# A graph layer with convolutions: output, hT and graph sums stored from GpSimd's queue, first batch's messages read in place

## The chip, the cores and the metric

The kernel runs on one core of one Trainium2 chip. The time is device microseconds (us) of one execution. The kernel before took a median of 2251.97 us over three runs (2245.11 to 2256.61). A profile is one further execution; all its numbers are that execution's.

The core's engines each work through their own list of instructions in order: TensorE (PE, matrix products; its weight loads are shown as PEld), VectorE (DVE), ScalarE (ACT), GpSimd (POOL) and SyncE (SP, which here only issues transfers). A transfer (DMA) is issued by an engine's queue and then moved by 16 DMA engines that all queues share.

## The reference

Input is x (32 batches of 512 nodes with 256 features) and an adjacency mask for each batch. Cut to what matters:

```python
h = maximum(layernorm(x), 0)                       # per node; h is called hT in the kernel, features on partitions
# inside the layer, with x = h:
c  = relu(conv1d(h, conv1_w, width 1) + bn1)
c  = conv1d(c, conv2_w, width 17) + bn2
x_conv = relu(c + h)
s   = h @ w_se.T + b_se                            # 3 numbers per node
A   = exp(-dist(s, s)) * adj
msg = relu(h @ w_msg.T + b_msg)
x_nmp = A @ msg                                    # the "graph sums"
gi = concat(x_conv, x_nmp) @ w_ih.T + b_ih
gh = h @ w_hh.T + b_hh
r, z = sigmoid(gi_r + gh_r), sigmoid(gi_z + gh_z)
n = tanh(gi_n + r * gh_n)
out = x + (1 - z) * n + z * h
```

## The kernel before, in words

All is float32. Work is divided into five streams, written as Python generators, and one planner that keeps a modelled clock `now` and, at each step, takes the next piece of the stream that is furthest behind its share. What a stream yields is the modelled time at which its next piece may go. The order in which pieces are taken is the order in which every engine's list is written; on the chip only semaphores hold an engine back.

- `begin(b)` and `norm`: layer-normalise x of batch b. DVE makes the statistics, GpSimd raises them to the power -0.5 (`rstd`, line 216), DVE makes `shift`, ACT applies both. Then `norm_t` turns the result by TensorE into hT, and stores hT to a DRAM tile (`HD`, shown as `hd`, line 318) from ACT's queue. Every later use of hT, except conv1 of the first four batches, loads it back on SP's queue: `hT` for conv1 (line 172), `hTg` for the messages (line 177), `hTb` for the gates (line 183).
- `rows(b)`: conv1, and its result into `h1` for a group of four batches (G = 4). A group's rows can be made only when the operands of the group before have been taken from `h1`.
- `convolution`: conv2 as 25 products per group of four batches, with transformed weights. These are kept in DRAM (`wd`) and loaded again for each group (`w`, line 469, three buffers).
- `graph(b)`: messages (`messages`), the factors of the distance, the exponential, the mask (`masked`; its rows of adj are loaded as `m_sb`, four transfers of 64 KB for each 128 rows from batch 8 on, line 264), and `gather`, which forms the graph sums and stores them to DRAM (`nd`, line 760) from ACT's queue.
- `gates(b)`: the gate products, and at the end `leave`, which turns the result, adds x (`res`, loaded by line 772) and stores the output in four transfers per half (line 892), from SP's queue. Each of them writes 32 partitions x 16 runs of 32 numbers (128 B).

Four facts about order matter below. First, each list is worked in order: while SP waits for one transfer's semaphore, every load behind it waits too. Second, every transfer is given one of eight semaphores in turn, `DMAHW0` to `DMAHW7` for those issued from SP and ACT together, `DMASW0` to `DMASW7` for those issued from GpSimd, and it waits until the transfer that had this semaphore last has landed. So a load on SP can be held by a store on ACT that stands some eight transfers earlier in the program, even if ACT has not reached that store yet. Third, `load` times in the planner are constants: it takes 6 us for a load of weights or rows. Fourth, at the start `graph(0)` loads `hTg` back from DRAM before the first messages can be formed.

Lines 127 and 132 are the helpers through which all products and turns by TensorE go, line 118 the one for DVE and ACT; they are told apart by tile names.

Of the kernel before, what the change touches and what calls it, by code (L numbers as in the profile page):

```python
# [44 lines left out]
def kernel(  # L45
# [28 lines left out]
    nc = tc.nc  # L74
# [23 lines left out]
    now = 5.0  # L98
    LAG = 0.6
# [22 lines left out]
    dve, act = Engine(nc.vector, 0.12, 0.00108), Engine(nc.scalar, 0.16, 0.0009)  # L122
# [6 lines left out]
    def turn(ps, a):  # L129
        nonlocal now  # L130
        now += 0.11
        nc.tensor.transpose(ps, a, ident)  # L132

    def matmul_sum(ps, pairs):
        for i, (lhsT, rhs) in enumerate(pairs):
            matmul(ps, lhsT, rhs, start=(i == 0), stop=(i == len(pairs) - 1))

    def bank():
        return gps.tile([P, N], F32, name="ps_g")
# [4 lines left out]
    def later(t, f):  # L144
        LATER.append((t, f))
        LATER.sort(key=lambda e: e[0])

    def settle():
        while LATER:
            LATER.pop(0)[1]()  # L150


    XS, HT, HB, HR, HG, XN, XR = {}, {}, {}, {}, {}, {}, {}
    NORMS, NORM_AT = {}, {}
    ARRIVES = (0.0, 7.0, 11.0, 13.0)
    HD = {b: dram.tile([P, ND, N], F32, name=f"hd{b}") for b in range(B)}
    ND_ = {(b, d): dram.tile([P, N], F32, name=f"nd{b}_{d}") for b in range(B) for d in range(ND)}
    begun = 0

    def fetch(b, xs=None):  # L160
        XS[b] = front.tile([P, NT, D], F32, name="x_sb", bufs=2) if xs is None else xs
# [2 lines left out]
    def load(b, xs=None):  # L164
        if b not in XS:
            fetch(b, xs)
        NORMS[b] = norm(b)
        NORM_AT[b] = now + 7.0 if b >= G else ARRIVES[b]

    def load_row(b):  # L170
        HR[b] = front.tile([P, ND, N], F32, name="hT", bufs=2)
        nc.sync.dma_start(HR[b], HD[b])

    def load_graph(b):
        if b < B and b not in HG and begun > b:
            HG[b] = front.tile([P, ND, N], F32, name="hTg", bufs=1)
            nc.sync.dma_start(HG[b], HD[b])
# [33 lines left out]
    def rsqrt(dst, var):  # L211

        n = dst.shape[-1]
        t = front.tile([P, 4], F32, name="veps")
        dve.tensor_scalar(t[:, :n], var, EPS, None, op0=ALU.add)
        nc.gpsimd.tensor_tensor(dst, t[:, :n], mhalf[:, :n], op=ALU.pow)
# [56 lines left out]
    def norm(b):  # L273

        xs = XS[b]
        st = front.tile([P, NT, 6], F32, name="st")
        mv = front.tile([P, NT, 2], F32, name="mv")
        for c in range(NT):
            dve.bn_stats(st[:, c, :], xs[:, c, :])
            dve.bn_aggr(mv[:, c, :], st[:, c, :])  # L280
            if c % 2:
                yield 0.0
        rstd = front.tile([P, NT], F32, name="rstd")
        rsqrt(rstd, mv[:, :, 1])
        yield dve.free + 1.5
        shift = front.tile([P, NT], F32, name="shift")
        dve.scalar_tensor_tensor(
            shift, mv[:, :, 0], -1.0, rstd, op0=ALU.mult, op1=ALU.mult
        )
        yield dve.free + 0.2  # L290
        for c in range(NT):
            act.activation(
                xs[:, c, :], xs[:, c, :], AF.Identity, bias=shift[:, c : c + 1],
                scale=rstd[:, c : c + 1],
            )
            if c % 2:
                yield act.free + LAG
# [10 lines left out]
    def norm_t(b, d):  # L308
        xn = XS[b]
        if d == 0:  # L310
            HT[b] = front.tile([P, ND, N], F32, name="hT", bufs=2)
        ps = bank()
        for c in range(NT):
            turn(ps[:, c * P : (c + 1) * P], xn[:, c, d * P : (d + 1) * P])
        act.activation(HT[b][:, d, :], ps, AF.Relu)
        if d == ND - 1:
            XS.pop(b)
            nc.scalar.dma_start(HD[b], HT[b])

    def conv1(b, o):  # L320
        hT = HT[b] if b < G else HR[b]
# [98 lines left out]
    WS, W_AT = [], []  # L420

    def new_w():
        return cv.tile([P, 3, ND, D], F32, name="w", bufs=3)
# [41 lines left out]
    def weights_again(m):  # L465

        w = new_w()
        k = 2 if m < 50 else 3
        nc.sync.dma_start(w[:, :k], WD[m % 25][:, :k])
        WS.append(w)  # L470
        W_AT.append(now + 6.0)

    thirds = set()

# [221 lines left out]
    def messages(b, msg, c):  # L696
        ps = bank()[:, : D + 3]
        matmul_sum(ps, [(HG[b][:, i, c * P : (c + 1) * P], wmsg[:, i, :]) for i in range(ND)])
        dve.tensor_tensor(msg[:, c, :], ps[:, :D], bmsg[:, :D], op=ALU.add)
        dve.tensor_tensor(gr.aug[:, c, :3], ps[:, D:], bmsg[:, D:], op=ALU.add)  # L700
        if c % 2:
            m = msg[:, c - 1 : c + 1, :]
            later(dve.free + 0.3, lambda: act.activation(m, m, AF.Relu))

    def factors():
        aug, augl = gr.aug, gr.augl
        sq = front.tile([P, NT, 3], F32, name="sq")
        dve.tensor_tensor(sq, aug[:, :, :3], aug[:, :, :3], op=ALU.mult)
        dve.tensor_reduce(aug[:, :, 4:5], sq, axis=mybir.AxisListType.X, op=ALU.add)
        dve.tensor_scalar(augl[:, :, :3], aug[:, :, :3], 2.0, None, op0=ALU.mult)  # L710
        dve.tensor_scalar(augl[:, :, 3:4], aug[:, :, 4:5], -1.0, None, op0=ALU.mult)
        dve.tensor_copy(
            gr.augr[:, :, :, :5], aug[:, :, None, :].to_broadcast([P, NT, 4, 5])
        )

    def factors_t():

        ps = bank()
        turn(ps[:, :P], gr.augl.rearrange("p c k -> p (c k)"))
        act.activation(gr.left, ps[:, :P], AF.Copy)  # L720
        ps = bank()
        for c in range(NT):
            turn(ps[:, c * P : (c + 1) * P], gr.augr[:, c].rearrange("p r k -> p (r k)"))
        act.activation(gr.right, ps, AF.Copy)
# [30 lines left out]
    def gather(b, msg, at, d):  # L755
        ps = bank()
        matmul_sum(ps, [(msg[:, c, d * P : (d + 1) * P], at[:, c, :]) for c in range(NT)])
        sums = gr.right if d == 0 else at[:, 0, :]
        act.activation(sums, ps, AF.Copy)
        nc.scalar.dma_start(ND_[b, d], sums)  # L760

# [17 lines left out]
    def begin(b):  # L781

        nonlocal begun
        yield lambda: b not in NORMS
        yield NORM_AT[b]
        for d in range(ND):
            norm_t(b, d)
            if d == ND - 1:
                begun = b + 1

                later_b = b + 4 if b < 2 else b + 2 if b >= G else B
                if later_b < B:
                    load(later_b)
            yield now
# [9 lines left out]

    def graph(b):

        yield lambda: begun > b
        if b not in HG:
            load_graph(b)
            yield now + 9.0  # L810
        msg = front.tile([P, NT, D], F32, name="msg", bufs=1)
        for c in range(NT):
            messages(b, msg, c)
            yield now
        factors()
        load_graph(b + 1)
        yield dve.free + LAG
        factors_t()
        if b < 1:
            yield lambda: begun >= G  # L820
        yield act.free + LAG
        at = front.tile([P, NT, N], F32, name="at", bufs=1)
        kernel_exp(at)
        yield act.free + 0.3
        for n in range(NT):
            masked(b, at, n)
            if n < NT - 1:
                yield dve.free - 0.2
        settle()
        yield dve.free + LAG  # L830
        for d in range(ND):
            gather(b, msg, at, d)
            yield now

    def gates(b):
# [49 lines left out]
        def leave(r, t, o, s):  # L885

            dve.transpose(t[:, s], r[:, s])
            y = XR[b, o]
            dve.tensor_tensor(y[:, s], t[:, s], y[:, s], op=ALU.add)
            for g in range(P // 32):  # L890
                at = slice(32 * g, 32 * g + 32)
                nc.sync.dma_start(
                    OB[b][:, s.start // 32 : s.stop // 32, o * P + 32 * g : o * P + 32 * g + 32],
                    y[at, s].rearrange("i (k j) -> i k j", j=32),
                )
            if s.stop == N:
                del XR[b, o]
                load_res(b + 1, o)

        for o in range(ND):  # L900
# [47 lines left out]
            for h in range(2):  # L948
                s = slice(h * N // 2, (h + 1) * N // 2)
# [58 lines left out]
    def all_rows():  # L1008
        nonlocal rows_wait
        for b in range(B):  # L1010
            if b < G:
                yield from begin(b)
                yield act.free + LAG
            else:
                yield lambda: freed >= b // G - 1 and begun > b
                rows_wait = True
                load_row(b)
                yield now + 6.0
            yield from rows(b)
            rows_wait = False  # L1020

# [119 lines left out]
```

## Time and profile before

| What | Value |
|---|---|
| Median of three runs | 2251.97 us (2245.11 to 2256.61) |
| The profiled execution's own time | 2247.76 us |
| Its span | 2246.0 us |
| Mean granted TensorE clock | 0.983 |
| PE busy | 2128.4 us, 95% of the span |
| DVE busy | 1494.8 us, 67% |
| ACT busy | 787.1 us, 35% |
| POOL busy | 56.0 us, 2% |

The profile lists busy time by engine, the chain of work that ended last (each step followed back to what released it), groups of equal instructions, waits (who waited for whom, total us, times, longest), and the transfers with their median time from issue to landing. "SPq" and "ACTq" are the queues in which those engines issue transfers. A line of the timeline begins with the start and the duration in us; in brackets at its end stands the idle time of that engine before it and what ended it.

### The profile page before, as it was taken

The page shows a single profiled execution, that of the slowest core. Times are in us where ns is not written, and L with a number is a line of the kernel's source. Part 1 is how long each engine was busy: PE and PEld are TensorE (multiplying, and loading weights), DVE is VectorE, ACT ScalarE, POOL GpSimd, SP SyncE. Part 2 cuts the span into 40 slices and gives each one's busy share as a digit, 9 for nine tenths or more (in the row PEclk, how much of TensorE's full clock was granted, in tenths as well). Part 3 has the DMA queues.
Part 4 walks back from the last instruction along what each step waited for, and adds up shares of the span by engine and source line. Part 5 has one row for each costly group of instructions (what it writes and reads, how often), then busy time and mean ns, then how long its engine had stood idle before and what let it go on. Part 6 is the DMA issues. An engine that isn't in the chain of part 4 may idle for free.

```text
span 2246.0 us, 26120 instructions
## 1 busy us (share of the span) xinstructions
PE 2128.4 (95%) x9392; PEld 1320.0 (59%) x9392; DVE 1494.8 (67%) x2770; ACT 787.1 (35%) x1323; POOL 56.0 (2%) x73
## 2 busy tenths in 40 slices
PE   5899899999989999899998999999999999999997
PEld 2677665566546665556565566656666566665443
DVE  4687876576746767567675686757767577776333
ACT  4445432433224341333432333332432324212311
POOL 1000000000000000000000000000000000000000
PEclk8899999999999999999999999999999999999999
DMA  5445756456554556455656446655656555553332
GB/s 218 150 151 187 245 172 183 122 163 175 150 150 143 155 171 176 133 141 150 172 161 181 126 135 176 176 185 147 166 152 165 127 162 154 153 168 85 70 66 38
DMA packets 563856, 342.42 MB, mean 152 GB/s; under 512 B 482512, under 2 KB 499280, under 8 KB 563088
## 3 DMA queue, kind: packets, MB, share of 16 engines
q1 hardware_dynamic: 544304, 287.54, 47.0%
q10 hardware_dynamic: 17424, 46.67, 5.3%
q0 software_dynamic: 2000, 6.56, 0.8%
q8 instruction: 74, 1.21, 0.2%
q14 instruction: 54, 0.44, 0.1%
HBM read 270.68 MB, written 69.99 MB: 152 GB/s over the span
## 4 chain that ended last, share of the span: by engine, by line
PE 85%; DMA 6%; DVE 4%; ACT 2%; issue 1%; SPq 1%; ACTq 0%; POOL 0%; DVEq 0%; POOLq 0%
PE ps_acc L127 41%; PE ps_g L127 19%; PE ps_c L127 15%; PE ps_b L127 6%; DMA w<-wd 2%; PE ps_g L132 2%; PE ps_b L732 1%; DMA hT<-hd 1%; DMA nd<-at 1%; DMA xnb<-nd 1%; DMA hd<-hT 1%; ACT at L118 1%; DVE gg L118 1%; DVE x L118 0%; DVE xconv L118 0%
## 5 line engine op out<-in xcount | busy, mean ns | idle before, releaser
L127 PE MATMUL ps_acc<-xconv,wih 128*128 128x512 f32 (+1 forms) x772 | 362.8, 592 | 5.7 <-ACT xconv L118 5.2
L127 PE MATMUL ps_acc<-xnb,wih 128*128 128x512 f32 (+1 forms) x772 | 362.9, 592 | 2.3 <-DMA xnb<-nd 2.3
L127 PE MATMUL ps_acc<-hTb,whh 128*128 128x512 f32 x768 | 355.7, 593 | 0.8 <-ACT r L118 0.8
L127 PE MATMUL ps_c<-xd,w 128*128 128x116 f32 x2800 | 342.6, 276 | 0.0
L127 PEld LDWEIGHTS ps_c<-xd,w 128*128 128x128 f32 x2800 | 328.5, 193 | 5.3 <-issue 5.3
L118 DVE TENSOR_TENSOR r<-ps_acc,r 128x512 f32<-128x512 f32 (+1 forms) x65 | 44.4, 683 | 385.6 <-PE ps_acc L127 385.6
L127 PEld LDWEIGHTS ps_acc<-xnb,wih 128*128 128x128 f32 x772 | 141.6, 189 | 165.3 <-issue 158.1
L127 PEld LDWEIGHTS ps_acc<-xconv,wih 128*128 128x128 f32 x772 | 141.5, 190 | 159.4 <-issue 147.3
L127 PE MATMUL ps_g<-at,msg 128*128 128x512 f32 x512 | 230.0, 599 | 4.1 <-DVE at L118 2.3
L127 PEld LDWEIGHTS ps_b<-x,w 128*128 128x128 f32 x1400 | 181.6, 192 | 87.8 <-issue 73.0
L127 PEld LDWEIGHTS ps_acc<-hTb,whh 128*128 128x128 f32 x768 | 141.2, 190 | 149.4 <-issue 144.4
L127 PE MATMUL ps_b<-x,w 128*128 128x116 f32 x1400 | 184.9, 275 | 23.4 <-DMA w<-wd 13.2
L118 ACT ACTIVATE mid<-ps_b 128x232 f32<-128x232 f32 x175 | 63.7, 364 | 359.4 <-PE ps_b L127 342.1
L127 PEld LDWEIGHTS ps_g<-at,msg 128*128 128x128 f32 x512 | 96.8, 192 | 119.4 <-issue 111.4
L127 PE MATMUL ps_g<-hT,w 128*128 128x512 f32 x256 | 126.7, 641 | 32.8 <-DMA hT<-hd 31.1
L118 DVE SCALAR_TENSOR_TENSOR x<-x,x 128x480 f32<-128x480 f32 (+1 forms) x184 | 144.1, 783 | 3.0
L127 PE MATMUL ps_g<-wmsg,hTg 128*128 128x259 f32 x512 | 130.4, 388 | 11.4 <-issue 10.9
L118 DVE TENSOR_TENSOR x<-x 128x240 f32<-128x240 f32 (+1 forms) x320 | 134.5, 463 | 0.4
L118 ACT ACTIVATE h<-ps_g,bn_shift,bn_scale 128x252 f32<-128x252 f32 (+1 forms) x192 | 81.0, 494 | 140.5 <-PE ps_g L127 140.1
L127 PEld LDWEIGHTS ps_g<-wmsg,hTg 128*128 128x128 f32 x512 | 96.7, 194 | 54.3 <-issue 41.7
L118 DVE TENSOR_TENSOR msg<-ps_g,bmsg 128x256 f32<-128x256 f32 x128 | 53.5, 420 | 107.1 <-PE ps_g L127 106.9
L118 DVE SCALAR_TENSOR_TENSOR r<-ps_acc,vec,r 128x512 f32<-128x512 f32 x64 | 48.0, 750 | 107.6 <-PE ps_acc L127 97.6
(100 smaller groups left out, 2420.5 us busy)
## 6 DMA issues: line engine op xcount, KB each, us to landing
w<-wd SPq DMA_DIRECT2D x150, 768.0 KB, 5.5
m_sb<-in_adj_dram SPq DMA_DIRECT2D x384, 64.0 KB, 2.5
hd<-hT ACTq DMA_DIRECT2D x32, 512.0 KB, 5.0
hTg<-hd SPq DMA_DIRECT2D x32, 512.0 KB, 4.1
res<-in_x_dram SPq DMA_DIRECT2D x256, 64.0 KB, 2.4
hTb<-hd SPq DMA_DIRECT2D x32, 512.0 KB, 5.9
xnb<-nd SPq DMA_DIRECT2D x64, 256.0 KB, 3.4
out_dram<-res SPq DMA_DIRECT2D x252, 64.0 KB, 2.0
```

The source lines that it names most:

```text
L118: getattr(self.engine, name)(*tiles, **more)
L127: nc.tensor.matmul(ps, lhsT, rhs, **more)
L132: nc.tensor.transpose(ps, a, ident)
L732: nc.tensor.matmul(pss[c], gr.left[k, :], gr.right[k, :], start=True, stop=True, tile_position=(32 * c, 0),)
```

## The change

Seven edits:

1. hT's store to `hd` and the graph sums' store to `nd` are issued from GpSimd's queue, no more from ACT's.
2. The output's stores are issued from GpSimd's queue, no more from SP's; and the planner issues them 0.4 us of its clock after the addition that they store has ended, no more together with it. The load of the next `res`, still on SP, follows them.
3. `graph(0)` reads `HT[0]`, the tile in SBUF, where it had loaded it back from DRAM.
4. So that this tile stays, `begin(2)` (the first to need its buffer) waits until the messages of batch 0 are written (`told`).
5. The planner expects `rstd` 2.0 us after the statistics (1.5 before).
6. It expects reloaded weights after 7.0 us (6.0 before).
7. It expects the reloaded rows of hT after 8.0 us (6.0 before).

```diff
-        yield dve.free + 1.5
+        yield dve.free + 2.0
...
-            nc.scalar.dma_start(HD[b], HT[b])
+            nc.gpsimd.dma_start(HD[b], HT[b])
...
-        W_AT.append(now + 6.0)
+        W_AT.append(now + 7.0)
...
-        nc.scalar.dma_start(ND_[b, d], sums)
+        nc.gpsimd.dma_start(ND_[b, d], sums)
...
     def begin(b):
         nonlocal begun
+        if b == 2:
+            yield lambda: told > 0
...
     def graph(b):
+        nonlocal told
         yield lambda: begun > b
-        if b not in HG:
+        if b == 0:
+            HG[0] = HT[0]
+            yield act.free + LAG
+        elif b not in HG:
             load_graph(b)
             yield now + 9.0
...
             messages(b, msg, c)
             yield now
+        told = b + 1
...
             dve.tensor_tensor(y[:, s], t[:, s], y[:, s], op=ALU.add)
+            later(dve.free + 0.4, lambda: store(y, o, s))
+
+        def store(y, o, s):
             for g in range(P // 32):
                 at = slice(32 * g, 32 * g + 32)
-                nc.sync.dma_start(
+                nc.gpsimd.dma_start(
                     OB[b][:, s.start // 32 : s.stop // 32, o * P + 32 * g : o * P + 32 * g + 32],
                     y[at, s].rearrange("i (k j) -> i k j", j=32),
                 )
             if s.stop == N:
                 del XR[b, o]
                 load_res(b + 1, o)
...
-                yield now + 6.0
+                yield now + 8.0
```

How the lists move is shown at three places. **TensorE at the start**, before; `hTg` is batch 0's hT loaded back, `ident` marks a turn, `w_182` is conv1's weight:

```order
L132 MATMUL ps_g<-ident,x_sb 128x128 x8
L127 MATMUL ps_g<-hT,w_182 128x512 x4
L132 MATMUL ps_g<-ident,x_sb 128x128 x8
L127 MATMUL ps_g<-wmsg,hTg 128x259 x6
L127 MATMUL ps_g<-hT,w_182 128x512 x4
L132 MATMUL ps_g<-ident,at 128x128 x8
```

and now:

```order
L132 MATMUL ps_g<-ident,x_sb 128x128 x8
L127 MATMUL ps_g<-hT,w_182 128x512 x4
L127 MATMUL ps_g<-wmsg,hT 128x259 x8
L132 MATMUL ps_g<-ident,x_sb 128x128 x8
L132 MATMUL ps_g<-ident,augl 128x128
L132 MATMUL ps_g<-ident,augr 128x128 x4
L127 MATMUL ps_g<-hT,w_182 128x512 x4
```

The messages of batch 0 moved ahead of batch 1's turns, and read `hT`.

**SP's list ahead of the load of batch 16's rows** (`hT<-hd_96`; the tiles `hd_80` to `hd_111` are batches 0 to 31), before, with the semaphores that each transfer waits for. Behind the last row shown stand seven more loads of `m_sb`, one of `w`, and then `hT<-hd_96`:

```order
L892 DMA out_dram<-res 32x16x32 [waits DMAHW3_49,DVE_49]
L892 DMA out_dram<-res 32x16x32 [waits DMAHW4_49]
L892 DMA out_dram<-res 32x16x32 [waits DMAHW5_49]
L892 DMA out_dram<-res 32x16x32 [waits DMAHW6_49]
L772 DMA res<-in_x_dram 32x16x32 [waits DMAHW0_49]
L772 DMA res<-in_x_dram 32x16x32 [waits DMAHW2_49]
L772 DMA res<-in_x_dram 32x16x32 [waits DMAHW3_49]
L772 DMA res<-in_x_dram 32x16x32 [waits DMAHW5_49]
L264 DMA m_sb<-in_adj_dram 32x16x32 [waits DMAHW6_49,DVE_49]
```

On ACT's list of before, the three stores issued about then have the semaphores 3, 6 and 0 in turn:

```order
L118 ACTIVATE right<-ps_g 128x512 [waits PE_49]
L760 DMA nd_0_128<-right 128x512 [waits DMAHW3_49,Activation_49]
L118 ACTIVATE hT<-ps_g 128x512 [waits PE_49] x2
L318 DMA hd_95<-hT 128x1024 [waits DMAHW6_49,Activation_49]
L118 ACTIVATE at<-ps_g 128x512 [waits PE_49]
L760 DMA nd_1_129<-at 128x512 [waits DMAHW0_49,Activation_49]
```

Now SP's list reads, at the same place (the same loads of `m_sb`, `w` and `hT<-hd_96` follow):

```order
L772 DMA res<-in_x_dram 32x16x32 [waits DMASW6_49,DMASW5_49,DMAHW4_49,DMASW4_49,DMASW3_49]
L772 DMA res<-in_x_dram 32x16x32 [waits DMAHW5_49]
L772 DMA res<-in_x_dram 32x16x32 [waits DMAHW6_49]
L772 DMA res<-in_x_dram 32x16x32 [waits DMAHW7_49]
L264 DMA m_sb<-in_adj_dram 32x16x32 [waits DMAHW0_49,DVE_49]
```

The output's stores left the list, and the stores of `hd` and `nd` no more share semaphores with the loads. The first `res` load waits for four stores of GpSimd's: those that last read its buffer, one half of a batch earlier than the four just issued.

**GpSimd's list** in the middle of the program held before only `rstd` (and, for the second group, stores of `wd`). It now reads, about batch 17 of `begin` and batch 10 of `graph`:

```order
L216 TENSOR_TENSOR rstd<-veps,mhalf 128x4 [waits DVE_49,Pool_49]
L318 DMA hd_97<-hT 128x1024 [waits DMASW6_49,Activation_49]
L902 DMA out_dram<-res 32x16x32 [waits DMAHW7_49,DMASW7_49,DVE_49]
L902 DMA out_dram<-res 32x16x32 [waits DMAHW0_49,DMASW0_49]
L902 DMA out_dram<-res 32x16x32 [waits DMAHW1_49,DMASW1_49]
L902 DMA out_dram<-res 32x16x32 [waits DMAHW2_49,DMASW2_49]
L760 DMA nd_0_132<-right 128x512 [waits DMASW3_49,Activation_49]
L760 DMA nd_1_133<-at 128x512 [waits DMASW4_49,Activation_49]
```

A round of one batch is four output stores, `rstd`, four output stores, and the stores of two sums and of one hT, all in one list.

More of the change, by code (lines that the diff above doesn't have):

```diff
@@ L157 @@
     ND_ = {(b, d): dram.tile([P, N], F32, name=f"nd{b}_{d}") for b in range(B) for d in range(ND)}
-    begun = 0
+    begun = told = 0
     def fetch(b, xs=None):
```

## The prediction, as put on record before the run

> **What bounds the kernel now.** I read the page first, for the bounding engine:
>
> ```profile
> span 2246.0 us, 26120 instructions
> ...
> PE 2128.4 (95%) x9392; PEld 1320.0 (59%) x9392; DVE 1494.8 (67%) x2770; ACT 787.1 (35%) x1323; POOL 56.0 (2%) x73
> ...
> PE 85%; DMA 6%; DVE 4%; ACT 2%; issue 1%; SPq 1%; ACTq 0%; POOL 0%; DVEq 0%; POOLq 0%
> ```
>
> TensorE has work for 2128.4 of 2246.0 us; 117.6 us are holes. The change takes no product away, so the holes, and what they do to TensorE's pace, are all that it can win. The chain of waits gives 6% of its length to transfers. The waits of PE alone name them (us, times, longest):
>
> ```profile
> PE ps_g L127 <- DMA hT<-hd: 31.1, 5, 9.9
> PE ps_b L127 <- DMA w<-wd: 13.2, 9, 3.4
> ...
> PE ps_g L127 <- issue: 10.9, 1, 10.9
> ...
> PE ps_acc L127 <- DMA xnb<-nd: 2.3, 3, 1.4
> ```
>
> Loads account for 31.1 + 13.2 + 2.3 = 46.6 us, and one hole of 10.9 us has no releaser in the profile. Of the rest, the first turn's start, some tens of short waits for ACT and DVE and the end are not touched.
>
> Next, why loads are late: the waits of SP's own queue.
>
> ```profile
> SPq L264 <- DVE right L118: 326.4, 62, 19.2
> SPq L892 <- DVE res L118: 263.7, 42, 15.3
> SPq L188 <- PE ps_acc L127: 129.1, 36, 13.5
> ...
> SPq L264 <- DMA nd<-right: 80.6, 9, 10.5
> SPq L892 <- DMA nd<-right: 72.8, 10, 9.6
> ...
> SPq L264 <- DMA hd<-hT: 21.5, 7, 7.4
> ```
>
> SP stood 263.7 us before output stores whose sum DVE had not made, and these three rows of store waits alone add 174.9 us in which a load or an output store waited for the semaphore of a store on ACT. All that time every load behind stood too. Whether that is what made PE wait is read at the hole itself. The three longest holes, in time order: for each, the SP waits of the stretch ahead of it, then the hole.
>
> ```profile
> SPq L892 <- DMA nd<-right: 9.5, 1, 9.5
> SPq L469 <- DMA nd<-at: 1.9, 1, 1.9
> ...
> 665.59 5.83 PE L127 MATMUL ps_g<-hT,w 128*128 128x512 f32 x8 [9.91 <-DMA hT<-hd]
> ```
>
> ```profile
> SPq L264 <- DMA nd<-right: 9.9, 1, 9.9
> SPq L264 <- DMA hd<-hT: 1.1, 1, 1.1
> SPq L264 <- DMA nd<-at: 1.0, 1, 1.0
> ...
> 941.96 3.75 PE L127 MATMUL ps_g<-hT,w 128*128 128x512 f32 x4 [7.48 <-DMA hT<-hd]
> ```
>
> ```profile
> SPq L892 <- DMA nd<-right: 9.6, 1, 9.6
> SPq L264 <- DMA hd<-hT: 5.8, 1, 5.8
> ...
> SPq L772 <- DMA nd<-at: 2.0, 1, 2.0
> ...
> 1216.53 5.15 PE L127 MATMUL ps_g<-hT,w 128*128 128x512 f32 x8 [7.83 <-DMA hT<-hd]
> ...
> 1227.72 3.61 PE L127 MATMUL ps_g<-hT,w 128*128 128x512 f32 x8
> ```
>
> SP lost 11.4, 12.0 and 17.4 us to stores on ACT ahead of holes of 9.91, 7.48 and 7.83 us: each loss is larger than its hole. In the third case the semaphores 3, 6 and 0 of the list shown above are the ones waited for. The last two rows show a second price: eight products right after the hole took 5.15 us, eight later ones 3.61.
>
> **The change part by part.**
>
> *Stores off SP and ACT (edits 1, 2).* Loads and stores no longer share semaphores, and no load stands behind an unfinished output any more. If every one of the holes on loads goes, that is 46.6 us; if none goes, because SP still waits for buffers (its rows L264 on DVE, 326.4, and L188 on PE, 129.1, stay), 0. The three holes above (25.2 us) are covered by waits that vanish. I take 41 and leave 5.6. The slower products behind the holes: 5.83, 5.15 and, for four, 3.75 us against 3.61 for eight give 2.2 + 1.5 + 1.9 = 5.6 us, and the shorter holes some more; I take 7 (0 to 9). ACT also loses 96 issues; it is 35% busy, so I count nothing.
>
> *What GpSimd's queue charges.* It gets 96 + 260 transfers more. The rows:
>
> ```profile
> out_dram<-res SPq DMA_DIRECT2D x252, 64.0 KB, 2.0
> ...
> nd<-right ACTq DMA_DIRECT2D x32, 256.0 KB, 2.0
> ...
> wd<-w POOLq DMA_DIRECT2D x25, 256.0 KB, 3.4
> ```
>
> ```profile
> L481 POOL DMA_DIRECT2D wd<-w x25: 539/539/731, 235.7 to 464.7; - x25
> ```
>
> ```profile
> L216 POOL TENSOR_TENSOR rstd<-veps,mhalf x32: 1006/1047/2276, 7.3 to 1659.8; 128x4 f32<-128x4 f32 x32
> ```
>
> ```profile
> L892 SPq DMA_DIRECT2D out_dram<-res x260: 315/488/2072, 313.4 to 2243.1; - x130
> ```
>
> ```profile
> L188 SPq DMA_DIRECT2D xnb<-nd x64: 319/344/1042, 246.1 to 2202.8; - x64
> ...
> L760 ACTq DMA_DIRECT2D nd<-at x32: 326/327/370, 102.2 to 2100.9; - x32
> ```
>
> A store that GpSimd issues now keeps it 0.54 us and lands 3.4 us after issue, where ACT's of the same size landed after 2.0. Those move 128 runs of 2 KB. An output store moves 512 runs of 128 B, which the trace never shows from GpSimd. Bounds: 0.54 us if the price is per transfer, 4 x 0.54 = 2.16 us if it is per run. A lower price has no reason; a higher one is the third rival. I take 1 us, nearer the first row, since even SP's 0.49 us per output store and ACT's 0.33 us for larger ones hardly follow the runs. Four stores then occupy 4 us (2.2 to 8.6), all together 260 us of a queue that is 2% busy.
>
> Who waits behind them? `rstd`, and DVE's `shift` behind that. Typical distances between the sum to be stored and the next `rstd`:
>
> ```profile
> 544.38 0.69 DVE L118 TENSOR_TENSOR res<-o_sb,res 128x512 f32<-128x512 f32 x1
> ...
> 558.52 1.05 POOL L216 TENSOR_TENSOR rstd<-veps,mhalf 128x4 f32<-128x4 f32 x1 [54.43 <-DVE sq L118]
> ```
>
> ```profile
> 1394.55 0.69 DVE L118 TENSOR_TENSOR res<-o_sb,res 128x512 f32<-128x512 f32 x1
> ...
> 1398.05 1.01 POOL L216 TENSOR_TENSOR rstd<-veps,mhalf 128x4 f32<-128x4 f32 x1 [55.64 <-DVE veps L118]
> ```
>
> From the sum's end to `rstd`: 13.5 and 2.8 us. Of the 20 such pairs after 350 us, 14 are as far apart as the first of these or farther. So 4 us rarely reach `rstd`, and some four or five times they delay it by 1 to 2 us, of which edit 5 has planned 0.5: +3 us in all on PE (0 to +10). A late `nd` is cheap: by the rows above, the first sum is loaded 144 us after its store and the last 102 us. The `res` load waits for stores half a batch, some 30 us, older.
>
> *The end.* The last output's eight stores are on the path:
>
> ```profile
> 2239.83 3.77 SPq L892 DMA_DIRECT2D out_dram<-res  x8
> ```
>
> SP issued eight in 3.77 us. GpSimd would need 8 x 0.54 = 4.3 to 8 us, and lands them 1.4 us later (3.4 against 2.0): +2 to +6, I take +3.
>
> *Messages read in place (edits 3, 4).* The hole without a releaser:
>
> ```profile
> 21.22 0.33 SPq L177 DMA_DIRECT2D hTg<-hd  x1
> ...
> 31.88 4.43 PE L127 MATMUL ps_g<-wmsg,hTg 128*128 128x259 f32 x12 [10.90 <-issue]
> ```
>
> PE stopped until the load issued at 21.22 had landed, 10.7 us later, with its weights and everything else there. Reading `hT` takes the load away. Since conv1 of all four batches and then the first operands follow in a row, the start shifts by the whole hole: -10.9. At best DVE, which stood as well, gains a little more (-13); at worst batch 2's and 3's statistics, now behind the messages' sums on DVE, give half of it back (-5). Holding back `begin(2)` costs nothing: the messages stand ahead of it on PE anyway.
>
> *Longer planned loads (edits 5 to 7).* They bring other work ahead of rows and weights; each can also open a short wait of another kind. With everything behind the start shifted, some short waits come anew: +6 (-5 to +15).
>
> **Sum**: -41 - 7 - 10.9 + 3 + 3 + 6 = -46.9 us. The profiled execution took 2247.76 us (span 2246.0), 4.2 us under the median of the runs; minus 46.9 that is 2200.9, and from the median 2205.1. I predict **2203**.
>
> **Rivals.**
>
> *A. Only the start is won.* SP's waits for buffers (326.4 and 129.1 us) stay; they could hold the same loads when the others go. Then -10.9 + 3 + 3, with a few of the load holes: about 2240. Against: the losses of 11.4, 12.0 and 17.4 us, none of them a buffer's. The Trainium skill ("DMA: Bandwidth & Descriptors", section "Issuing engines are not separate DMA queues") says that transfers started by several engines run on the same DMA engines, and that starting them on several saves only the issue time; by that rule this rival is what would happen. The trace does not bear it out for this kernel, since its 9.5 us waits are waits in the queue.
>
> *B. Level.* The load holes go, but short waits of DVE and ACT take their place, since those had time to run ahead during the holes: -46.9 + 40, about 2243 to 2255. For it: the chain of waits gives DVE 4% and ACT 2% already. Against: at 67% and 35% busy neither is near a bound.
>
> *C. Slower: output stores keep GpSimd long.* The mechanism: four stores take longer than the typical 13.5 us to the next `rstd`, and DVE then stands at `shift` with all operands of conv2 behind it. It decides from 13.5 / 4 = 3.4 us a store. At 6 us, `rstd` comes 24 - 13.5 = 10.5 us late, 20 times: 210 us for DVE, whose idle third takes 70, and of the rest PE loses perhaps half: 70 us against -46.9, so about 2270. For it: no row shows 128 B runs from GpSimd. Against: 0.54 us for 128 runs, so 3.4 us needs a price per run 57% above the most that this row can hold.
>
> **Chances.** Forecast (-20 to -70 us) 0.63; A 0.12; B 0.11; C 0.14. The forecast's own range is 2178 to 2232; with A and most of B the range is 2176 to 2250. About 0.5% (11 us) is what a measurement of this kernel can tell from no change. Faster by more (below 2240.7): the forecast and two thirds of A, 0.71. Within: 0.15. Slower (C): 0.14.
>
> **What would show it.** PE's waits for `hT<-hd` and `w<-wd` under 10 us together, from 44.3; no hole near 21 us, and the first conv2 product near 53 instead of 64.28; SP's waits for `nd` and `hd` gone; GpSimd's output stores at about 1 us each, its busy time about 370 us (56 + 260 x 1 + 96 x 0.54). The step on GpSimd is wrong if DVE's wait of `shift` for `rstd` is far above 10 us; the step on loads is wrong if holes on `hT<-hd` stay though SP waits for no store. A time above 2250 would mean rival C.

## The result, and the profile after

The changed kernel takes 2177.36 us (median of four runs, 2173.9 to 2180.12) beside 2249.04 us of the kernel before on the same chip (four runs, 2245.11 to 2256.61): a ratio of 0.9677, 95% interval 0.9644 to 0.9709. The gain is 71.7 us where 46.9 were forecast; the time lies 1.4 us above the lower end of the range (2176), and 0.6 us below the 2178 where the forecast's own range ended.

The profiled execution took 2179.13 us, with a span of 2177.0. The page of after, its span and busy time:

```profile
span 2177.0 us, 26672 instructions
...
PE 2113.7 (97%) x9392; PEld 1314.7 (60%) x9392; DVE 1494.1 (69%) x2770; ACT 784.4 (36%) x1323; POOL 282.9 (13%) x429
```

The span fell by 69.0 us. PE's holes went from 117.6 to 2177.0 - 2113.7 = 63.3 us (-54.3), and its busy time by 14.7 for the same 9392 products. The waits of PE alone (total us, times, longest) show which holes are left:

```profile
PE ps_g L132 <- ACT x_sb L118: 9.9, 5, 9.2
PE ps_g L127 <- DVE at L118: 7.7, 3, 5.8
PE ps_g L732 <- ACT hT L118: 6.6, 1, 6.6
...
PE ps_g L132 <- DMA m_sb<-in_adj_dram: 0.7, 1, 0.7
```

The rows `hT<-hd` (31.1), `w<-wd` (13.2), `xnb<-nd` (2.3) and `issue` (10.9) are gone; the last row shown is the only wait of PE for a transfer that is left. SP's own waits:

```profile
SPq L264 <- DVE right L118: 359.0, 70, 19.2
SPq L188 <- PE ps_acc L127: 354.1, 58, 20.6
...
SPq L172 <- DMA hd<-hT: 23.8, 3, 8.3
```

SP stands as long as before (some 1540 us over all its rows before, 1610 now), now mostly for buffers. No row names `nd`, and the last one is the load of rows waiting for its own data to land in `hd`, not for the store of another batch. So long waits on SP are not bad in themselves: here the waits for buffers hold loads that still come in time.

Where the 69.0 us lie is read from four stretches that hold nearly the same products, cut at the first conv2 product, some 170 us later, and at the last group's gates. The columns are the stretch, its length, busy time and number of instructions of PE, PEld, DVE, ACT and POOL, the granted TensorE clock, the share of the DMA engines, and GB/s. Before:

```profile
0.00:64.00 64.00, 33.18 (x101) 17.21 (x101) 34.63 (x105) 33.99 (x70) 9.99 (x22) 0.85 0.60 228
64.00:236.00 172.00, 160.02 (x1069) 133.40 (x1069) 131.94 (x251) 82.78 (x156) 5.25 (x5) 0.96 0.45 162
236.00:2110.00 1874.00, 1813.62 (x7937) 1115.27 (x7937) 1284.41 (x2350) 650.07 (x1070) 40.73 (x47) 0.99 0.56 156
2110.00:2246.00 136.00, 121.63 (x289) 54.11 (x287) 43.83 (x67) 20.23 (x28) 0.00 (x0) 0.98 0.28 54
```

After:

```profile
0.00:53.00 53.00, 31.88 (x101) 16.85 (x101) 35.07 (x106) 34.56 (x70) 14.51 (x27) 0.92 0.68 254
53.00:225.00 172.00, 158.41 (x1072) 130.58 (x1071) 127.94 (x240) 81.72 (x155) 11.24 (x15) 0.98 0.50 176
225.00:2038.00 1813.00, 1800.33 (x7929) 1112.44 (x7930) 1285.87 (x2358) 647.80 (x1070) 231.91 (x347) 1.00 0.58 160
2038.00:2177.00 139.00, 123.11 (x292) 54.80 (x292) 45.20 (x68) 20.27 (x28) 25.29 (x40) 0.98 0.27 52
```

The start is 11 us shorter, the next stretch equal, the long middle 61 us shorter and the end 3 us longer (of which some 1.3 are three more products). In the middle PE's holes fell from 60.4 to 12.7 us, and nearly as many products (8 fewer) took 13.3 us less at a higher clock.

What GpSimd pays, in the groups of its instructions (busy us, mean ns) and in the transfers' landing (median us from issue):

```profile
L902 POOL DMA_DIRECT2D out_dram<-res x260 | 169.0, 656 | 1005.0 <-DVE res L118 889.2
...
out_dram<-res POOLq DMA_DIRECT2D x252, 64.0 KB, 3.3
```

An output store costs GpSimd 0.65 us, near the lower bound of 0.54.

### The profile page after: what moved, and what is told of

It reads as the page before. It is cut to its first block, busy times and chain, and to the rows that moved or that the text cites. A ratio compares the mean times of both kernels' runs of the same rounds, so it can differ in the third digit from the quotient of the medians.

```text
span 2177.0 us, 26672 instructions
## 1 busy us (share of the span) xinstructions
PE 2113.7 (97%) x9392; PEld 1314.7 (60%) x9392; DVE 1494.1 (69%) x2770; ACT 784.4 (36%) x1323; POOL 282.9 (13%) x429
## 2 busy tenths in 40 slices
DMA packets 432709, 341.94 MB, mean 157 GB/s; under 512 B 351424, under 2 KB 368192, under 8 KB 431936
## 4 chain that ended last, share of the span: by engine, by line
PE 58%; issue 31%; DVE 4%; POOL 3%; ACT 2%; DMA 2%; ACTq 0%; POOLq 0%; SPq 0%; DVEq 0%
PE ps_acc L127 25%; PE ps_g L127 14%; PE ps_c L127 12%; PE ps_b L127 5%; POOL out_dram L902 3%; PE ps_g L132 2%; DMA x_sb<-in_x_dram 1%; PE ps_b L732 1%; DVE x L118 1%; DVE g L118 1%; POOL nd L760 0%; ACT y L118 0%; DVE gg L118 0%; DVE at L118 0%; DVE z L118 0%
## 5 line engine op out<-in xcount | busy, mean ns | idle before, releaser
L902 POOL DMA_DIRECT2D out_dram<-res x260 | 169.0, 656 | 1005.0 <-DVE res L118 889.2
L127 PEld LDWEIGHTS ps_b<-x,w 128*128 128x128 f32 x1400 | 182.8, 192 | 68.9 <-issue 53.4
L127 PE MATMUL ps_g<-wmsg,hTg 128*128 128x259 f32 x496 | 124.3, 382 | 0.0
L127 PE MATMUL ps_g<-hT,w 128*128 128x512 f32 x256 | 118.2, 605 | 5.2 <-ACT hT L118 4.1
L118 DVE TENSOR_TENSOR xd<-x 128x480 f32<-128x480 f32 x175 | 113.8, 651 | 4.2 <-PE ps_c L127 4.1
```

The costliest lines, as they stand in the source:

```text
L118: getattr(self.engine, name)(*tiles, **more)
L127: nc.tensor.matmul(ps, lhsT, rhs, **more)
L902: nc.gpsimd.dma_start(OB[b][:, s.start // 32 : s.stop // 32, o * P + 32 * g : o * P + 32 * g + 32], y[at, s].rearrange("i (k j) -> i k j", ...
```

## Experiments: which of the moved stores mattered

All times below stand beside runs of the kernel before on the same chip (its medians there: 2255.3, 2252.91 and 2255.6 us for the three series), so the ratios are what is compared. Two theories: **shared semaphores** (loads on SP wait for `hd` and `nd` stores that stand late on ACT) and **unfinished outputs** (loads stand on SP behind output stores whose sum is not made). The prediction held both at once. In the expectations they are theory 1 or S, and theory 2 or O; the two together are the queue theory, and its rival, the **order** theory, says that the gain comes from the shifted order and the planner's new constants.

**Both kinds of store moved back**, the other edits kept:

```diff
-            nc.gpsimd.dma_start(HD[b], HT[b])
+            nc.scalar.dma_start(HD[b], HT[b])
...
-        nc.gpsimd.dma_start(ND_[b, d], sums)
+        nc.scalar.dma_start(ND_[b, d], sums)
...
-                nc.gpsimd.dma_start(
+                nc.sync.dma_start(
```

The last hunk is the issue of the output's stores.

> The changed kernel with hd and nd stored from ACT and the output from SP again; the start, the constants and the later issue of the output's stores stay. Queue theory: the waits of loads come back, PE waits 25 us or more for hT<-hd and w<-wd, time 2215 to 2240. Order theory: about 2190, holes on loads under 15 us.

Measured: 2227.51 us, ratio 0.9877 [0.9862, 0.9892]. **Only the output's stores back on SP** (the last of these three hunks alone):

> The changed kernel with only the output's stores back on SP (still issued when due); hd and nd stay on GpSimd. Theory 1 (the shared semaphores are the larger part: a load on SP waits for a store that ACT has not reached): SP's waits for nd and hd gone, its waits for DVE res near 245 us, few holes on loads, 2185 to 2197. Theory 2 (the larger part is SP standing in order before unfinished outputs): 2205 to 2220, as bad as with both back (2227).

Measured: 2174.84 us, ratio 0.9652 [0.9626, 0.9677]. **Only the stores of hd and nd back on ACT** (the first two hunks alone):

> The changed kernel with only hd and nd back on ACT; the output's stores stay on GpSimd. Theory 1 (shared semaphores): SP waits 250 us or more for nd and hd, PE's holes on hT<-hd and w<-wd 20 us or more, 2200 to 2220. Theory 2 (order behind unfinished outputs): 2180 to 2190.

Measured: 2197.87 us, ratio 0.9749 [0.9719, 0.978]. With the changed kernel these make a square:

| | output on SP | output on GpSimd |
|---|---|---|
| hd, nd on ACT | 0.9877 (2227.5 us) | 0.9749 (2197.9 us) |
| hd, nd on GpSimd | 0.9652 (2174.8 us) | 0.9677 (2177.4 us) |

With hd and nd off ACT, it makes no difference that can be measured where the output's stores are. SP's waits with the output on SP and hd, nd on GpSimd:

```profile
SPq L902 <- DVE res L118: 270.3, 42, 13.3
...
SPq L172 <- DMA hd<-hT: 24.3, 3, 8.4
```

SP stands 270.3 us before unfinished outputs, more than the 263.7 of before, and no hole of PE on `hT<-hd`, `w<-wd` or `xnb<-nd` is left. The reading that these 263.7 us make loads late was wrong here. A rival would be that the loads land faster once the stores of hd and nd leave ACT's queue. The rows' loads do not (KB each, median us from issue to landing; both moved back, then only the output):

```profile
hT<-hd SPq DMA_DIRECT2D x28, 512.0 KB, 5.3
```

```profile
hT<-hd SPq DMA_DIRECT2D x28, 512.0 KB, 5.2
```

They are not moved faster but issued earlier: near 640 us, one of them is issued 9.7 us (628.55) behind the start of the output stores ahead of it (618.83), where with both kinds moved back it is 20.3 us (644.11 and 623.77). With hd and nd left on ACT, moving the output's stores is worth 0.0128 (29 us), although hd and nd still share semaphores with the loads. SP's waits in that kernel:

```profile
SPq L772 <- DMA nd<-right: 73.1, 10, 9.5
SPq L264 <- DMA nd<-right: 71.9, 9, 9.9
```

The waits for `nd` stay. PE's holes on loads fall only in part: `hT<-hd` from 18.3 us with both moved back to 10.6, `w<-wd` from 13.3 to 0.2, together 20.8 of the 29 us, and PE's busy time by 10.3 (2131.2 to 2120.9). So the second theory holds too as long as hd and nd stand on ACT. The two gains overlap: from both moved back, the output's move alone wins 0.0128, that of hd and nd alone 0.0225, and both together 0.0200, no more than the larger one.

The order theory fails as the account of the main gain (0.9652 and 0.9877 belong to kernels with the same edits 3 to 7, which differ only in the queue that issues hd and nd), yet with both moved back the kernel is still faster than before, by 0.0123: edits 3 to 7 and the later issue of the output's stores win something there.

The version with the output left on SP is as fast as the changed kernel with fewer edits; no version tried is faster by more than the intervals allow.

**Edit 1 alone in the kernel before**, two lines:

```diff
-            nc.scalar.dma_start(HD[b], HT[b])
+            nc.gpsimd.dma_start(HD[b], HT[b])
...
-        nc.scalar.dma_start(ND_[b, d], sums)
+        nc.gpsimd.dma_start(ND_[b, d], sums)
```

> The kernel before with edit 1 alone: the stores of hd and nd issued from GpSimd, nothing else. Theory S (shared semaphores of hd and nd are the cause, the output's stores on SP are not): nearly all of what edits 1 and 2 won together (-65.2 us) comes back, 2185 to 2200 us; SP still waits over 200 us before output stores for DVE res, and TensorE's waits on hT<-hd and w<-wd fall under 8 us together. Theory O (unfinished outputs on SP hold the loads too, as the prediction had it): 2210 to 2235 us, with hT<-hd still at 10 us or more.

Measured: 2202.13 us, ratio 0.9763 [0.9741, 0.9785]. **Edits 1 and 2 in the kernel before**, without the start and the three constants:

> The kernel before with edits 1 and 2 alone (hd, nd and output stored from GpSimd, the output's stores when due), the start and the planner's constants as before. Queue theory: PE's waits for loads under 10 us together, first conv2 product still near 64 us, time about 2190 (-59). Order theory: the constants of 6 us are then too short, holes on hT<-hd and w<-wd stay at 25 us or more, time 2215 or more.

Measured: 2187.68 us, ratio 0.9707 [0.9686, 0.9727]. So two lines bring some 53 of the 72 us (0.0237 of 0.0323); the time lies just above the band of the first theory and below that of the second. Edit 2 adds 0.0056 (about 13 us) on this base, where it added nothing above. PE has no row for `w<-wd` with edit 1 alone; its row for `hT<-hd` (11.5 us, 2.0 with edit 2 added), and SP and PE about its largest such hole:

```profile
PE ps_g L127 <- DMA hT<-hd: 11.5, 5, 4.3
```

```profile
1178.83 2.95 SPq L892 DMA_DIRECT2D out_dram<-res  x4
1181.82 2.11 SPq L772 DMA_DIRECT2D res<-in_x_dram  x4
1184.10 0.37 SPq L172 DMA_DIRECT2D hT<-hd  x1
```

```profile
1188.12 5.19 PE L127 MATMUL ps_g<-hT,w 128*128 128x512 f32 x8 [4.32 <-DMA hT<-hd]
```

Here the second theory is true in small: SP stood 4.7 us before the output stores, for `res` of DVE, then issued them and four `res` loads, and the rows' load behind them came 4.32 us late. In the kernel with the output on SP and edits 3 to 7, the same three rows stand in the same order 18 us earlier (output stores at 1160.53), and PE has no hole on them. Edit 7 gives the rows' load 2 us more of the planner's clock, which fits, but edits 3 to 7 came together there; that it is edit 7 is not shown.

**Which of hd and nd.** From the kernel with the output on SP, hd's stores put back on ACT (only nd's on GpSimd), and the reverse:

```diff
-            nc.gpsimd.dma_start(HD[b], HT[b])
+            nc.scalar.dma_start(HD[b], HT[b])
```

```diff
-        nc.gpsimd.dma_start(ND_[b, d], sums)
+        nc.scalar.dma_start(ND_[b, d], sums)
```

> The changed kernel with the output's stores back on SP and hd's store back on ACT: only nd's 64 stores are on GpSimd. With both back the time was 2227.5 us, with neither of hd and nd back 2174.8. SP's waits there were 168 us and more for semaphores of nd and some 20 for hd. Theory S by size of SP's waits: nd alone wins about 45 of the 52.7 us, 2178 to 2190 us. If what counts is instead the hd stores, which stand right ahead of the loads of the rows and are larger (512 KB): 2205 to 2225 us.

> The changed kernel with the output's stores back on SP and nd's stores back on ACT: only hd's 32 stores are on GpSimd. Theory S by size of SP's waits: little is won, 2210 to 2225 us, and SP's waits for semaphores of nd stay at 130 us or more. If hd's stores are what counts: 2180 to 2195 us.

Measured: nd alone on GpSimd 2206.39 us, ratio 0.9785 [0.9755, 0.9815]; hd alone 2222.58, ratio 0.9853 [0.9829, 0.9878]. Of 52.7 us between neither and both (0.0225 in ratio), nd alone brings 21.1 (0.0092) and hd alone 4.9 (0.0024, which is within the intervals): about half together. The size of SP's waits foretold 45 for nd, and that was wrong. That hd's stores are what counts is no better: nd alone would fit it (2205 to 2225), but hd alone would then have had to bring 2180 to 2195. Why both fail is seen at the hole of PE that ends at 649.45 us with neither moved and at 642.67 with nd alone moved. SP's waits for stores on ACT in the 28 us ahead of it, with neither moved (a hole of 6.87 us):

```profile
SPq L902 <- DMA nd<-right: 9.5, 1, 9.5
SPq L469 <- DMA nd<-at: 1.9, 1, 1.9
...
SPq L772 <- DMA hd<-hT: 0.2, 1, 0.2
```

and with nd alone on GpSimd (a hole of 5.54 us):

```profile
SPq L772 <- DMA hd<-hT: 9.8, 1, 9.8
```

ACT issues this `hd` store at 628.27 us, and SP takes from 620.37 until 632.06 for the four `res` loads that wait for it. Summed over all lines of SP's waits:

| kernel (edits 3 to 7 in each) | SP waits for nd, us (times) | for hd, a load's own data included, us (times) | time, us |
|---|---|---|---|
| output on SP, neither of hd, nd moved | 257.7 (47) | 63.3 (17) | 2227.5 |
| only hd moved | 274.3 (49) | 8.0 (1), its own data | 2222.6 |
| only nd moved | 0 | 162.8 (17) | 2206.4 |
| both moved | 0 | 24.3 (3), its own data | 2174.8 |

SP waits for hd 17 times with or without nd on ACT, but 9.6 us each time in place of 3.7: where no `nd` holds it first, it arrives earlier at the next late store. At this hole one late member of the shared ring is enough: the waits of `nd` and `hd` do not add up, and in the table the loads are free only when both are gone. That the delay moves from `nd` to `hd` is what the rows show; beyond this hole the ring's members were not followed transfer by transfer.

## Experiments: the start, the constants, the delay

**The start alone** (edits 3 and 4 in the kernel before):

```diff
+        if b == 2:
+            yield lambda: told > 0
...
+        if b == 0:
+            HG[0] = HT[0]
+            yield act.free + LAG
+        elif b not in HG:
```

> The kernel before with edits 3 and 4 alone (messages of batch 0 read in place, begin(2) held back). Queue theory (holes on loads come from stores in the queues of SP and ACT): the start is won and nothing else, first conv2 product near 53 us instead of 64.28, PE's waits for hT<-hd and w<-wd still 35 to 50 us together, time about 2238 (-11). Rival (order theory: the gain of the middle comes from the shifted order and the planner's new constants, not from the queues): with another order the holes change too, so 2210 to 2260 without a rule.

Measured: 2250.52 us, ratio 0.9985 [0.9972, 0.9998]. The first conv2 product starts at 55.80, 8.5 us earlier, and nearly all is given back at 242 us; PE's waits for loads stay (`hT<-hd` 33.2 us, `w<-wd` 14.5), as the queue theory had it. SP's list there, and PE:

```profile
221.50 13.01 SPq L772 DMA_DIRECT2D res<-in_x_dram  x8
...
236.25 1.58 SPq L261 DMA_DIRECT2D m_sb<-in_adj_dram  x3
```

```profile
241.95 1.09 PE L132 MATMUL ps_g<-ident,m_sb 128*128 128x128 f32 x4 [16.09 <-DMA m_sb<-in_adj_dram]
```

The earlier schedule writes a load of the mask behind eight loads of `res`, which take SP 13.01 us, and PE stops 16.09 us for it. So the gain at the start is real but needs the loads behind it in the right order.

**The constants back** (edits 5 to 7 undone, 1 to 4 kept):

```diff
-        yield dve.free + 2.0
+        yield dve.free + 1.5
...
-        W_AT.append(now + 7.0)
+        W_AT.append(now + 6.0)
...
-                yield now + 8.0
+                yield now + 6.0
```

> The changed kernel with the planner's constants of before (1.5, 6 and 6 us instead of 2, 7 and 8). Queue theory: loads now land in time anyway, 2172 to 2186, waits of PE for loads under 10 us. Order theory: 2195 or more, with holes on hT<-hd again.

Measured: 2185.86 us, ratio 0.969 [0.9669, 0.9711]. The same hole is there:

```profile
PE ps_g L132 <- DMA m_sb<-in_adj_dram: 13.9, 1, 13.9
```

In the changed kernel one load of the mask stands ahead of the eight `res` loads (218.14 against 219.72 us), and 0.7 us of this wait is left, with a new one of 5.84 us for DVE behind it. The profiled spans differ by 8.1 us (2185.1 and 2177.0), but the ratios 0.969 and 0.9677 overlap: the hole is shown, the worth of the constants as a time is not settled. They were no cost, at least. With the stores in their old queues they are worth more: the kernel with both kinds moved back (0.9877) differs from that with the start alone (0.9985) by edits 5 to 7 and the later issue of the output's stores, and there the wait for the mask falls from 16.1 us to 0.7 and that for `hT<-hd` from 33.2 to 18.3. That fits a planner that leaves loads more time and so hides a part of the same waits; which of these edits does it is not shown.

**The output's stores not put off by 0.4 us:**

```diff
-            later(dve.free + 0.4, lambda: store(y, o, s))
+            store(y, o, s)
```

> The changed kernel, but the output's four stores and the next res load are put in the lists together with the addition, not 0.4 us of the planner's clock later. GpSimd does nothing else for long, so if its queue is no bound this changes nothing: 2172 to 2184, GpSimd's waits for DVE res a little longer. If the later issue matters, 2190 or more, with DVE's waits of shift for rstd above 30 us.

Measured: 2176.83 us, ratio 0.966 [0.9635, 0.9686]: no difference from the changed kernel.

## Experiments: how long GpSimd may take

Fills of a tile that nobody uses, behind each four output stores, make GpSimd's list longer and touch nothing else:

```diff
+            for _ in range(64):
+                nc.gpsimd.memset(gr.augr2, 0.0)
```

> The changed kernel with 64 small fills of an unused tile on GpSimd behind every four output stores, which should keep it 10 to 13 us longer each time (about 15 us for a group instead of 2.6). The prediction's third rival said that GpSimd may be kept for 13.5 us a group before rstd comes late: then DVE's waits of shift for rstd stay under 60 us and the time within 15 us of 2177. If the margin is smaller than the rows of before suggested, 2200 or more.

Measured: 2217.47 us, ratio 0.9842 [0.9815, 0.9869], 40 us above the changed kernel, and DVE's wait of `shift` for `rstd` is 75.6 us, 15 times: both beyond what was expected. Read only from the time, this says that the margin of GpSimd is far smaller than thought. The timeline of GpSimd at the end says something else:

```profile
2152.78 2.58 POOL L903 DMA_DIRECT2D out_dram<-res  x4 [0.40 <-issue]
2155.35 13.30 POOL L908 MEMSET idle<- 128x64 f32 x64
...
2201.60 2.30 POOL L903 DMA_DIRECT2D out_dram<-res  x4 [0.38 <-issue]
2203.89 13.30 POOL L908 MEMSET idle<- 128x64 f32 x64
```

and DVE's last sum, in the same kernel:

```profile
2183.41 0.42 DVE L118 TENSOR_TENSOR res<-o_sb,res 128x256 f32<-128x256 f32 x1
```

and in the changed kernel:

```profile
2169.67 0.42 DVE L118 TENSOR_TENSOR res<-o_sb,res 128x256 f32<-128x256 f32 x1
```

A group takes 2.58 + 13.30 + 0.40 = 16.3 us, and in the last groups GpSimd, with nothing but groups one behind the other, falls behind by itself: some 29 of the 42 us of span come after the last sum. Only 13.7 us were lost before it. (The fills leave DVE's own work as it was: busy 1493.8 us beside 1494.1.) So the dose was taken up again, larger and without the end (112 fills, none for the last four batches):

```diff
+            for _ in range(112 if b < 28 else 0):
+                nc.gpsimd.memset(gr.augr2, 0.0)
```

> The changed kernel with 112 fills of an unused tile behind each four output stores of batches 0 to 27, none for the last four batches: by the 0.208 us that a fill took with 64 of them (13.3 us), a group keeps GpSimd 2.6 + 23.3 + 0.4 = 26.3 us, against 16.3 us with 64. There the last sum was 13.7 us later than in the changed kernel, and the other 28 us were GpSimd alone at the end, which the missing fills exclude here. The third rival's own arithmetic (a delay of 26.3 - 13.5 = 12.8 us 20 times, less DVE's idle 70, half of the rest on TensorE): +93 us, about 2270 us. If the delays fall into slack as with 64 fills and grow only in proportion to the fills: +24 us, about 2201 us. GpSimd's waits rstd <- DVE and DVE's shift <- rstd should show it: over 200 us for DVE's if the first holds.

Measured: 2327.56 us, ratio 1.032 [1.0296, 1.0343]: slower than the kernel before, and above what either expectation gave (93 and 24 us over the changed kernel; it is 150). GpSimd's list, and DVE behind it (the bracket: what it waited):

```profile
709.47 2.62 POOL L903 DMA_DIRECT2D out_dram<-res  x4 [9.05 <-DVE res L118]
712.08 23.30 POOL L908 MEMSET idle<- 128x64 f32 x112
735.34 1.04 POOL L216 TENSOR_TENSOR rstd<-veps,mhalf 128x4 f32<-128x4 f32 x1
```

```profile
736.41 0.16 DVE L118 SCALAR_TENSOR_TENSOR shift<-mv,rstd 128x4 f32<-128x4 f32 x1 [16.76 <-POOL rstd L216]
```

In total, of DVE and of PE:

```profile
DVE shift L118 <- POOL rstd L216: 219.6, 20, 23.0
...
PE ps_g L132 <- ACT x_sb L118: 50.7, 16, 9.2
```

DVE's wait is 208 us above the changed kernel's 11.6, and the span 147.4 us longer (2324.4 against 2177.0): 106.4 us more of PE's holes, and 41.0 us more for the same products at a mean clock of 0.966 in place of 0.992. The mechanism of the third rival is real: at 16.3 us a group 13.7 us before the last sum, at 26.3 us 147. Between the two the loss grows by some 13 us for each us that a group is longer. The changed kernel's 2.6 us lie far below.

## Why the prediction was right, and where its steps were not

- **The direction, and what bounds the kernel.** Right. Loads that came late made the holes, and they are gone: the 46.6 us fell to none, with 0.7 us for a load of the mask, where the sum took 41. The three large holes were laid to stores on ACT, by SP's losses of 11.4, 12.0 and 17.4 us ahead of them; the runs with hd and nd alone moved bear it out (0.9652 beside 0.9877, no such hole left, loads that land no faster). Not tried are stores that stay on ACT with semaphores of their own: that it is the semaphores and not ACT's queue itself is read from SP's rows, and followed at one hole only.
- **"No load stands behind an unfinished output any more."** Not needed for the changed kernel's gain: with the output back on SP, SP stands 270.3 us there, no hole on those loads comes, and the time is the same. It has a price where other edits are missing: 0.0128 with hd and nd on ACT, and 0.0056 in the kernel before with edit 1. A long wait in SP's list was read as harm without following it to a hole, which the prediction itself had asked for and done only for the stores on ACT.
- **The slower products behind holes, -7.** The mechanism is right, the size is not: busy time fell by 14.7 us. (It is known to some 4 us: the version with the output on SP has the same holes and 2109.8 us in place of 2113.7.) In the second of its three lines the prediction read four products that the stretch shown had cut off from their eight; those eight took 5.88 us, which makes the three holes 6.0 us, not 5.6. Conv1's 256 products, on which the `hT<-hd` holes lay, fell from 126.7 us to 118.2, near the 7 taken; the rest lay where the term did not look, with 3.0 us on the products `ps_c<-x,w` of the first conv2 and 2.4 on the messages. The granted clock of before around the first of these holes (same columns as above) shows what is behind it:

```profile
640.00:655.00 15.00, 15.00 (x57) 8.19 (x56) 12.43 (x18) 2.65 (x5) 0.00 (x0) 1.00 0.40 93
655.00:666.00 11.00, 1.09 (x8) 0.94 (x7) 0.00 (x0) 0.00 (x0) 0.00 (x0) 0.71 0.86 271
666.00:672.00 6.00, 6.00 (x10) 2.35 (x10) 0.00 (x0) 1.81 (x5) 0.00 (x0) 0.67 0.32 128
672.00:680.00 8.00, 8.00 (x26) 4.06 (x25) 2.45 (x4) 2.56 (x7) 0.00 (x0) 1.00 0.31 99
```

  The clock is 1.00 before the hole, 0.71 in it and 0.67 in the 6 us behind it. So this hole cost its length and then some 2 us of products at a lower clock. All runs together hold 37 holes on `hT<-hd` with eight products right behind them. Behind the 14 of 0.34 to 2.85 us these eight took 3.67 to 3.70 us, behind the 22 of 2.95 to 10.46 us they took 5.15 to 6.70, and one of 1.99 us, with 5.40, does not fit. So a hole of 3 us costs its length and another 1.5 to 3 us, and a hole of 10 us not much more than that besides its length. The hole at the start, which the term had not counted, shows it too: the start's 101 products took 33.18 us before at 0.85, and 31.88 now at 0.92. The Trainium skill ("TensorE: Matmul & The Clock Gate", section "Part 1: The HAM clock gate (the "warmup" mystery)") says that the array falls to half rate after an idle window of about 3.4 us and is released after as much work; the trace agrees with that in kind, with 0.67 as the mean over the 6 us and the change near 2.9 us of hole.
- **The start, -10.9.** Right: 64.28 to 53.16, that is -11.1 (the forecast position was 53). By the first row of the stretches 9.7 us of it are holes and 1.3 pace: the hole of 10.9 is gone, and new short waits for `hT` take a little of it. That the gain is kept was luck in part: alone, it was given back at 242 us behind eight `res` loads, a mishap that none of the steps had looked for.
- **GpSimd's price.** 0.65 us a store, 1 was taken, within the bounds 0.54 to 2.16; GpSimd is busy 282.9 us where about 370 were forecast. Of the 20 distances from a sum to the next `rstd` 12, not 14, are as long as the 13.5 us or longer (14 from 12.9 us on), which changes nothing at 2.6 us a group. `rstd` late, +3: DVE's wait for it rose from 6.0 to 11.6 us, and no hole of PE shows it; the term is 0 as far as can be seen. The end, +3: the first of the last eight stores is issued 7.4 us before the span's end now, against 6.2; the stretch, without its three more products, shows +1.7.
- **New short waits, +6.** The remaining holes grew by some 1 us beside the end (54.3 less of holes, of which 45.9 are loads and 10.9 the start, so +2.5 in all). The longer planned loads were no cost.
- **The sum.** The misses have one sign: loads 5, pace 8, `rstd` 3, the end 1.5, short waits 5, together 22.5 of the 22.1 us (by rounding) between -46.9 and the span's -69.0. Each cost was taken from the middle of its bounds although most rows spoke for the low end. That the time still lies inside the range is luck, by 1.4 us: it was widened for A and B, which are slower than the forecast.
- **Rivals.** A (only the start) is out: two moved lines, without the start, bring a ratio of 0.9763, and the start alone 0.9985. B (level) did not happen. C is a mechanism that exists but was too cheap in the prediction: +93 worked out for 26.3 us a group, +147 measured; that it begins at 13.5 us a group is not shown, only that 2.6 us are clear of it and 16.3 us are not. The Trainium skill's rule that several issuing engines save only issue time ("DMA: Bandwidth & Descriptors", section "Issuing engines are not separate DMA queues"), by which A would have come, does not cover this kernel. The two lines with their 0.9763 end waits in a queue.

## What to carry to other kernels

When loads come late, look in the issuing queue's waits for stores of another engine: transfers that take semaphores in turn from one ring can wait for its slowest member. Here all late stores had to leave the ring, and moving one kind of them showed only a part of the gain. Follow each long wait in a load queue to a hole of the bounding engine before counting it; with hd and nd moved, 270 us of SP waiting cost nothing. Causes that delay the same load do not add up, so try them one by one and together. A probe that makes an engine slower has to be read stage by stage, since the end of the program pays for it in another way than the middle.

## What was not expected of the hardware

- The same output stores need far fewer packets from GpSimd: 563856 packets in all before, 432709 after. Against the kernel that differs only in the output's stores on SP, GpSimd's queue has 8320 more of them, 32 for each of the 260 stores, and SP's 135232 fewer, some 520 for each store; a full store has 512 runs. The queues' rows (packets, MB, share of 16 engines) with the output on SP:

```profile
q1 hardware_dynamic: 544160, 287.02, 49.4%
q0 software_dynamic: 11728, 40.12, 4.7%
```

  and of the changed kernel:

```profile
q1 hardware_dynamic: 408928, 270.23, 45.0%
q0 software_dynamic: 20048, 56.91, 8.4%
```

  The two shares sum to 54.1% and 53.4% of spans of 2172.6 and 2177.0 us: far fewer packets, about the same time of the DMA engines.
- GpSimd's issue price hardly follows the number of runs: 0.65 us for 512 runs of 128 B against 0.54 us for 128 runs of 2 KB. A store lands 3.3 us after its issue, against 2.0 from SP.
